# Attention's row sums from a further weight column and squares on ScalarE, last choices of 12 and 8 tiles, and a residual written from SBUF

## The chip, the cores and the metric

The kernel runs on one core of a Trainium2 chip. The metric is the time of one launch on the device, in microseconds (us): the median of several runs, as measured beside the runs of other kernels on the same chip. One execution is also recorded by the hardware profiler; the profile tables below come from that one.

## What is computed

The reference is a "macaron" block on x of 4 x 2048 tokens with 256 features, in float32: a mixture-of-experts layer, an attention layer and the same mixture again, each on a layer norm of its input and each added to x.

```python
x = x + 0.5 * ffn(layernorm(x), router_w, wg, wu, wd)
x = x + attn(layernorm(x), Wq, bq, Wk, bk, Wv, bv, Wo, bo)
x = x + 0.5 * ffn(layernorm(x), router_w, wg, wu, wd)

# attn: 16 heads of 16; the keys are a softmax of q, and k's projection is unused
q = softmax(heads(x @ Wq + bq), -1) * s
k = softmax(q, axis=-2) * s              # over the tokens
out = (q @ (k^T v)) @ Wo + bo            # a 16x16 context per head

# ffn: 8 experts, each token to its best 2, at most 1280 tokens per expert by weight
logits = x @ router_w.T ; top 2 of softmax, weights made to sum to 1
out[token] += weight * ((silu(x @ wg[e]) * (x @ wu[e])) @ wd[e])
```

## The kernel before

The 8192 tokens are 64 tiles of 128 (T = 64, 16 tiles per batch). The program has five stages that follow one another: a first router with its route (to about 113 us), the first experts (to 893), attention with the second router (to 1137), the second route (to about 1197), the second experts (to 1989). Each engine works through its own instructions in order. In the routers, routes, experts and attention that order is written out by hand for TensorE (PE), VectorE (DVE), ScalarE (ACT) and GpSimd (POOL), by the order of the calls; the transfers on SyncE's queue (SP) are placed by the scheduler.

**First router and route.** `first_router` (L1156) loads x into `xw` (128 partitions, 64 tiles, 280 columns: 256 of x, 8 of weights, 16 factors), computes each tile's logits and, for all 64 tiles at once, the choice of two experts (`choose`, L191). `write_rows` (L257) writes the rows of 280 to DRAM, from which the experts later gather. `route` (L260) finds for each expert the weight at which its capacity is reached, by 30 bisection steps of 1.32 us that pass between VectorE (L291, L296 to L298) and TensorE (L290, L292), and then the slot of each token: two scans on VectorE (L310, L319), one product (L320), four transposes on TensorE ("back", L326), and shifts (L328 to L335). Ahead of these transposes stand 14 filler matmuls of 128 columns (`stay_busy`, L158, called in L323), which wait for nothing but the matmuls before them. `RowList` (L357 to L416) turns the slots of the first expert into a list of rows, and GpSimd gathers them (L470). The first instruction of `RowList` on VectorE (L357, "hi") writes memory that the router's tiles held, so it waits for all transfers out of them. The first layer's residual, `acc`, is set to x by four transfers from DRAM to DRAM (L1245), and the experts' results are added to it.

**Experts.** Each of 16 chunks runs some 640 matmuls of 128x320 (L561, L764); TensorE is busy throughout. They start when the first rows are gathered.

**Attention** (L916). `acc` is loaded into `xw` in pairs of tiles, and a loop of 44 steps (L1105, LAST = 44) handles a pair of tiles at several ages in each step. In step i, by the order of calls:
- `project` and `largest` of pair i-1: q = x Wq by 8 matmuls ("qp", L949), scaled and shifted on VectorE (L957), its maxima (L962), its router columns copied (L963), the maxima subtracted on GpSimd (L964). The right-hand side has W1 = 264 columns: 256 of Wq and 8 of the router, so that the router's logits of x come with q.
- `keys` of pair i-3 (ScalarE, L981 twice, L983), `exp` and `share` of pair i-2 (ScalarE L967; sum and reciprocal on VectorE, L971 and L973; product on GpSimd, L974).
- `stats` of pair i+1 for attention's own layer norm (VectorE L933, L934; GpSimd L169, L170).
- `turn_q` of pair i-3 and `turn_x` of pair i: four transposes each on TensorE (L992, L941) and a copy on ScalarE (L994, L943).
- `add_y` of pair y = i-12: attention's output by 8 matmuls of 264 columns ("py", L1062), again with the router's logits.
- `sums` of pair i-3: products of keys and x over the batch's tokens, 8 matmuls ("pc", L1004).
- `choose_on`: a few instructions of a choice that is under way, then `take_y` (L1070): the output is added to `xw` on VectorE (L1072), both tiles get their statistics (L1074), every second pair is stored, and every second pair `norm_of` (L172) turns the statistics of four tiles into `rstd` and `shift`: four small VectorE instructions (L182 to L185), and on GpSimd `deviation` (L169, L170) and three more (L187 to L189). When a group of tiles is complete, its choice is queued.

After each batch (16 tiles, 8 pairs) `context_1` to `context_4` turn the sums into a matrix that maps q to the output: a reciprocal on VectorE (L1015), scalings (L1017, L1018), transposes ("trg", L1026), products ("ctx", "mops"). The groups of choices are 16, 16, 12, 16 and 4 tiles. In the last 8 steps only outputs and choices are left. Two PSUM buffers take turns for the outputs there.

The places that the change touches, with what is fixed by hand in them:

```python
            for n in (NJ, NJ, NJ - 4, NJ, 4):                                   # L1083, NJ = 16
...
                if i < LAST - PB - 2:                                           # L1145, PB = 8
                    choose_on(2)
                if has(y):
                    take_y(y, ps)
                if i >= LAST - PB:
                    choose_on({LAST - 3: 0, LAST - 2: 5, LAST - 1: 3}.get(i, 4))
            while choosing:
                for k in reversed(range(len(choosing))):
                    choose_on(1, k)
```

The whole functions:

Of the kernel before, what the change touches and what calls it, by code (L numbers as in the profile page):

```python
# [9 lines left out]
F32 = mybir.dt.float32  # L10
# [4 lines left out]
ALU = mybir.AluOpType  # L15
# [12 lines left out]
def macaron_kernel(  # L28
# [129 lines left out]
    def stay_busy(ps, n, cols=BANK):  # L158

        for _ in range(n):  # L160
            nc.tensor.matmul(ps[:, :cols], ident, row_of_ones[:, :cols], start=True, stop=True)
# [4 lines left out]
    def deviation(var, n, pool, dst, scale=1.0):  # L166

        ve = pool.tile([P, NJ], F32, tag="ve", name="ve", bufs=4)
        nc.gpsimd.tensor_scalar(ve[:, :n], var, scale, EPS, ALU.mult, ALU.add)  # L169
        nc.gpsimd.tensor_tensor(dst, ve[:, :n], spread(minus_half, [P, n]), ALU.pow)  # L170
# [89 lines left out]
    def route(w, pool, ppool, beside=iter(())):  # L260

        FULL = [P, GT * P]

        def new(name, dtype=F32):
            return pool.tile(FULL, dtype, name=name)

        def one(name, dtype=F32, n=1):
            return pool.tile([P, n], dtype, name=name)  # L270

        ps = ppool.tile([P, GT, P], F32, tag="turn", name="turn", bufs=1)
        by_group = w.rearrange("p e (g r) -> p r (e g)", r=GT)
        for r in range(GT):
            nc.tensor.transpose(ps[:, r, :], by_group[:, r, :], ident)
        wt = new("wt")
        nc.vector.tensor_copy(wt, ps.rearrange("p r q -> p (r q)"))

        cand, low, high = one("cand", I32), one("low", I32), one("high", I32)
        cand_f = cand.bitcast(F32)
        part = one("part", F16)
        above, tie = new("above", F16), new("tie", F16)
        nc.vector.memset(cand, 1 << 29)
        for bit in range(29, -1, -1):

            reach = ppool.tile([P, 4], F32, tag="cnt", name="reach", bufs=2)
            nc.tensor.matmul(reach[:, :1], group4, short, start=True, stop=False)  # L290
# [24 lines left out]
        nc.vector.tensor_tensor(need_t, need, cnt[:, 2:3], ALU.subtract)  # L315
        nc.vector.scalar_tensor_tensor(off, off, float(-1 - NOWHERE), cnt[:, 1:2], ALU.add, ALU.add)
        nc.vector.scalar_tensor_tensor(tie, St, need_t, tie, ALU.is_le, ALU.mult)
        nc.vector.tensor_tensor(above, above, tie, ALU.add)
        nc.vector.tensor_tensor_scan(St, row_of_ones, above, 0.0, ALU.mult, ALU.add)  # L319
        nc.vector.scalar_tensor_tensor(St, St, off, above, ALU.add, ALU.mult)  # L320


        stay_busy(ppool.tile([P, GT, P], F32, tag="turn", name="turn", bufs=1)[:, 0, :], 14, P)  # L323
        ps = ppool.tile([P, GT, P], F32, tag="turn", name="back", bufs=1)
        for r in range(GT):
            nc.tensor.transpose(ps[:, r, :], St[:, r * P : (r + 1) * P], ident)  # L326
        slot = pool.tile([P, E * T], I16, name="slot")
        nc.vector.tensor_scalar(  # L328
            slot.rearrange("p (q r) -> p q r", r=GT), ps.rearrange("p r q -> p q r"),
            float(NOWHERE), None, ALU.add,  # L330
        )
        nc.vector.tensor_scalar(
            slot_hi.rearrange("p e t -> p (e t)"), slot, 7, None, ALU.logical_shift_right
        )
        nc.vector.tensor_scalar(slot_lo.rearrange("p e t -> p (e t)"), slot, P - 1, None, ALU.bitwise_and)  # L335
        nc.gpsimd.tensor_scalar(behind_lo, slot_lo, -1.0, 0.5, ALU.mult, ALU.add)
# [509 lines left out]
                if i0 + CH == ST:  # L846
                    load_expert(e + 2, wpool, weights)

    W1 = D + E

    att_weights = []

    def attention_weights(pool, ppool):
# [18 lines left out]
        nc.sync.dma_start(out=boT, in_=bo.rearrange("(c p) -> p c", p=P))  # L872
        nc.sync.dma_start(out=box[:, 0:D], in_=bo.partition_broadcast(P))
        yield
        nc.gpsimd.tensor_copy(wqx[:, :, D:], wrx[:, :, :E])
        for w in (wqx[:, :, 0:D], wvx):
            ps = ppool.tile([P, 2 * D], F32, tag="turn", name="means", bufs=1)
            for c in range(DC):
# [17 lines left out]
        for k in range(DC):  # L896
            for c in range(DC):
                nc.tensor.matmul(
                    ps[:, k * E : (k + 1) * E], woT[:, c, k * P : (k + 1) * P], wqx[:, c, D:],
                    start=(c == 0), stop=(c == DC - 1),  # L900
                )
            yield
        nc.scalar.copy(wox[:, :, D:], ps[:, : DC * E].rearrange("p (k e) -> p k e", k=DC))
        yield
        ps = ppool.tile([P, 2 * D], F32, tag="turn", name="bor", bufs=1)
        for c in range(DC):
            bob = pool.tile([P, P], F32, tag="bob", name="bob", bufs=2)
            nc.scalar.mul(bob, ones, boT[:, c : c + 1])
            nc.tensor.matmul(ps[:, :E], bob, wqx[:, c, D:], start=(c == 0), stop=(c == DC - 1))
            yield  # L910
        nc.scalar.mul(box[:, D:], ps[:, :E], 1.0 / H)
        nc.gpsimd.tensor_scalar(box[:, 0:D], box[:, 0:D], 1.0 / H, None, ALU.mult)
        nc.gpsimd.tensor_scalar(mask, heads, QSCALE * QSCALE, None, ALU.mult)
        att_weights.extend((wqx, wvx, wox, bqs, bvT, box, mask))
# [1 line left out]
    def attention(xw, w, to, weights, pool, ppool):  # L916
# [3 lines left out]
        PB = NJ // 2  # L920
        NP = T // 2
        xT, qp, qs, zs, eks, qT, mo, pcs = {}, {}, {}, {}, {}, {}, {}, {}
        st3 = pool.tile([P, T, 6], F32, name="st3")
        ring = []
        for k in range(4):
            r = pool.tile([P, 2, D + 1], F32, name=f"xs{k}")
# [143 lines left out]
        def take_y(i, ps):  # L1070
            xs = xw[:, 2 * i : 2 * i + 2, 0:W1]
            nc.vector.tensor_tensor(xs, xs, ps[:, :, 0:W1], ALU.add)  # L1072
            for t in (2 * i, 2 * i + 1):
                nc.vector.bn_stats(st3[:, t, :], xw[:, t, 0:D])  # L1074
            t = 2 * i + 2 - JL
            if t % JL == 0:
                stored.append(nc.sync.dma_start(out=out_tiles[:, t : t + JL, :], in_=xw[:, t : t + JL, 0:D]))
            if i % 2:
                norm_of(st3, slice(2 * i - 2, 2 * i + 2), pool)


            stop = 0
            for n in (NJ, NJ, NJ - 4, NJ, 4):  # L1083
                stop += n
                if 2 * i + 2 == stop:
                    ts = slice(stop - n, stop)
                    choosing.append((ts, choose(xw, w, ts, pool)))

        def choose_on(n, which=0):

            while len(choosing) > which and n:
                ts, steps = choosing[which]
                n -= 1
                if next(steps, 0) == 0:
                    write_rows(xw, to, ts)
                    choosing.pop(which)

        def has(i, n=NP):
            return 0 <= i < n

        LAST = NP + PB + 4
        with tc.manual_schedule(engines=ENGINES):
            stay_busy(ppool.tile([P, 2, 2 * D], F32, tag="py", name="py", bufs=1)[:, 0, :], 7)
            stats(0, 2)
            for i in range(LAST):  # L1105
# [38 lines left out]
                    sums(i - 3)  # L1144
                if i < LAST - PB - 2:  # L1145
                    choose_on(2)
                if has(y):
                    take_y(y, ps)
                if i >= LAST - PB:

                    choose_on({LAST - 3: 0, LAST - 2: 5, LAST - 1: 3}.get(i, 4))
            while choosing:
                for k in reversed(range(len(choosing))):
                    choose_on(1, k)
# [57 lines left out]
    with tc.tile_pool(name="w1", bufs=2) as wpool:  # L1212
        weights, ws = {}, {}
        with tc.tile_pool(name="r1", bufs=1) as pool, tc.tile_pool(name="r1p", bufs=2, space=PSUM) as ppool:
# [5 lines left out]
            with tc.manual_schedule(engines=ENGINES):  # L1220
# [14 lines left out]
                steps = attention_weights(pool, ppool)  # L1235
                next(steps)
                first_router(xw, w, pool, ppool)
                for b in range(B):
                    write_rows(xw, rows[0], slice(b * NJ, (b + 1) * NJ))
                steps = chain(weight_sums(nc.gpsimd, 0, wpool, weights, ws, 0, 1), steps)  # L1240
                route(w, pool, ppool, steps)
                for _ in steps:
                    pass
        for b in range(B):
            nc.sync.dma_start(out=acc[b * N : (b + 1) * N, :], in_=x_in[b])  # L1245
        load_expert(1, wpool, weights)

        with tc.tile_pool(name="f1", bufs=1) as pool, tc.tile_pool(name="f1p", bufs=2, space=PSUM) as ppool:
# [55 lines left out]
```

## Time and profile before

| what | before |
|---|---|
| median of 3 runs | 1992.83 us (1991.8 to 1993.83) |
| profiled execution, its time | 1991.23 us |
| profiled execution, span of the instructions | 1989.5 us |
| busy: PE / DVE / ACT / POOL | 93% / 70% / 46% / 52% of the span |
| first rows gathered, first and second experts | 113.6 us, 1199.6 us |
| start of attention, start of the second route | 897.6 us, 1136.9 us |
| statistics of the outputs (DVE L1074) | 64 instructions, 24.1 us busy |
| TensorE's clock | 0.50 from 36.5 to 97.9 us and from 1128.8 to 1183.4 us, mostly 1.00 otherwise |

The span runs from the first instruction to the last; the execution's own time is 1.7 us longer. "Busy" is the time in which an engine had an instruction in work; a busy TensorE need not be at full speed, since its clock is granted in steps of one half and one. In a row of instructions the two numbers are the start and the length; "xN" merges N in a row, and where instructions overlap in the pipeline a single one's length is longer than the distance to the next one. In brackets stands how long the engine was idle ahead of it, and which work ended that wait. A chain follows from the last instruction back to what released each one.

### The profile page before, as it was taken

Reading aid. Unit: us, or ns where it says so; the run is one execution under the profiler, and the core shown is the slowest. Engines: PE = TensorE matmul, PEld = TensorE weight load, DVE = VectorE, ACT = ScalarE, POOL = GpSimd, SP = SyncE. Lnnn points to the kernel's source line nnn. Section 1 sums busy time; section 2 is a strip of 40 time slices with the busy share of each in tenths; the row PEclk is TensorE's granted clock in tenths of the full one; section 3 lists DMA queues with packets and bytes.
Section 4 is the critical chain, followed back from the end, with each engine's and each line's share of the span. In section 5 each row is a group of like instructions: output and inputs, shape, how many; then the busy total and the mean of one; then the engine's idle time right before and its main releaser. Section 6 shows DMA issues by size and latency. Waiting matters only on the chain.

```text
span 1989.5 us, 25361 instructions
## 1 busy us (share of the span) xinstructions
PE 1843.9 (93%) x8812; PEld 1341.8 (67%) x8812; DVE 1386.9 (70%) x2539; ACT 922.4 (46%) x2269; POOL 1031.8 (52%) x1019
## 2 busy tenths in 40 slices
PE   6479999999999999999999528999999999999997
PEld 5347777777777777777888425777777777777776
DVE  7856767676767676647788885676767666676763
ACT  5045455555646463325444105554646373737332
POOL 4335555555555555535556324555555555555552
PEclk8589999999999999999999858999999999999999
DMA  9911323222222221125012541222222223232121
GB/s 339 332 30 28 92 34 86 59 61 71 50 71 49 71 50 28 28 25 172 25 40 89 187 142 29 71 50 71 49 71 50 71 50 79 41 95 30 31 29 19
DMA packets 99936, 148.85 MB, mean 75 GB/s; under 512 B 7512, under 2 KB 86368, under 8 KB 99680
## 3 DMA queue, kind: packets, MB, share of 16 engines
q1 hardware_dynamic: 69072, 103.29, 15.3%
q0 software_dynamic: 30720, 43.93, 13.8%
q8 instruction: 70, 1.15, 0.3%
q14 instruction: 58, 0.48, 0.1%
q10 hardware_dynamic: 16, 0.01, 0.0%
HBM read 99.49 MB, written 56.10 MB: 78 GB/s over the span
## 4 chain that ended last, share of the span: by engine, by line
PE 88%; DVE 6%; issue 3%; POOL 1%; ACT 1%; DMA 1%; POOLq 0%; DVEq 0%; ACTq 0%; SPq 0%
PE mm L561 49%; PE mm L764 23%; PE qp L949 2%; PE pc L1004 2%; PE tr L496 2%; PE py L1062 2%; PE back L716 2%; DVE above L291 2%; PE ix L396 1%; PE mm L822 1%; PE tr L1168 1%; DVE cand L298 1%; PE trq L992 1%; PE trx L941 1%; PE lg L1177 0%
## 5 line engine op out<-in xcount | busy, mean ns | idle before, releaser
L561 PE MATMUL mm<-xs,ws 128*128 128x320 f32 x1536 | 476.9, 433 | 2.8 <-DVE u L502 1.8
L505 POOL TENSOR_TENSOR ct<-ct 128x320 f32<-128x320 f32 x360 | 339.6, 943 | 187.9 <-DVE ct L592 164.4
L561 PEld LDWEIGHTS mm<-xs,ws 128*128 128x128 f32 x1536 | 284.3, 190 | 111.9 <-DVE u L502 2.9
L502 DVE TENSOR_TENSOR ct<-u,mm 128x640 f32<-128x640 f32 x256 | 209.9, 820 | 177.2 <-PE mm L561 166.0
L502 DVE TENSOR_TENSOR ct<-ct,mm 128x640 f32<-128x640 f32 x288 | 236.0, 819 | 73.7 <-PE mm L561 72.8
L470 POOL DMA_INDIRECT r<-rows,ixs x160 | 156.9, 981 | 235.2 <-ACT eo L697 172.8
L764 PE MATMUL mm<-ct,wds 128*128 128x320 f32 x960 | 278.1, 432 | 0.0
L589 ACT ACTIVATE ct<-ct 128x960 f32<-128x960 f32 (+2 forms) x192 | 141.7, 738 | 293.1 <-DVE ct L502 293.1
L390 ACT ACTIVATE lo<-from_below,behind_lo 128x129 f16<-128x129 f32 x896 | 272.9, 396 | 0.0
L764 PEld LDWEIGHTS mm<-ct,wds 128*128 128x128 f32 x960 | 179.2, 190 | 72.0 <-DVE ct L502 3.3
L764 PE MATMUL mm<-ct,wdt 128*128 128x320 f32 x720 | 213.5, 433 | 0.0
L698 POOL DMA_INDIRECT acc<-eo,ixs x80 | 127.7, 1596 | 142.9 <-ACT eo L697 124.9
L698 POOL DMA_INDIRECT out_dram<-eo,ixs x80 | 127.6, 1595 | 142.9 <-ACT eo L697 124.9
L561 PE MATMUL mm<-xsT,wgt 128*128 128x320 f32 x512 | 184.8, 443 | 0.0
L561 PE MATMUL mm<-xsT,wut 128*128 128x320 f32 x512 | 180.7, 435 | 0.0
L592 DVE TENSOR_TENSOR ct<-ct 128x640 f32<-128x640 f32 (+1 forms) x128 | 160.8, 1256 | 21.7 <-ACT ct L589 21.7
L502 DVE TENSOR_TENSOR u<-p,mm 128x640 f32<-128x640 f32 x128 | 105.1, 821 | 93.0 <-PE mm L561 80.6
L764 PEld LDWEIGHTS mm<-ct,wdt 128*128 128x128 f32 x720 | 132.1, 190 | 47.5
L561 PE MATMUL mm<-xsT,ws 128*128 128x320 f32 x512 | 158.7, 432 | 0.0
L598 ACT COPY p<-mm 128x640 f32<-128x640 f32 x128 | 88.4, 690 | 147.1 <-PE mm L561 147.1
L697 ACT ACTIVATE eo<-back,r 128x256 f32<-128x256 f32 x150 | 64.9, 478 | 152.7 <-PE back L716 152.7
L561 PEld LDWEIGHTS mm<-xsT,wut 128*128 128x128 f32 x512 | 97.7, 191 | 40.7 <-issue 0.8
(234 smaller groups left out, 2803.7 us busy)
## 6 DMA issues: line engine op xcount, KB each, us to landing
wgt<-in_L_ffn_wg_dram SPq DMA_DIRECT2D x16, 1024.0 KB, 4.9
wut<-in_L_ffn_wu_dram SPq DMA_DIRECT2D x16, 1024.0 KB, 7.2
wdt<-in_L_ffn_wd_dram SPq DMA_DIRECT2D x16, 1024.0 KB, 5.4
rows<-xw SPq DMA_DIRECT2D x7, 2240.0 KB, 19.4
xw<-in_L_attn_x_dram SPq DMA_DIRECT2D x16, 512.0 KB, 9.3
out_dram<-xw SPq DMA_DIRECT2D x16, 512.0 KB, 2.9
xw<-acc SPq DMA_DIRECT2D x15, 512.0 KB, 8.6
r<-rows,ixs POOLq DMA_INDIRECT x160, 2.8
```

Source lines behind the costliest of these rows:

```text
L291: nc.vector.tensor_scalar(above, wt, cand_f, 0.0, ALU.is_ge, ALU.add, accum_out=part)
L390: nc.scalar.activation(lo[:, t, :], from_below, AF.Sign, bias=at, scale=1.0)
L470: nc.gpsimd.indirect_dma_start(out=r, out_offset=None, in_=src[:, :], in_offset=bass.IndirectOffsetOnAxis(ap=lists[e][:, i : i + 1], axis=0),)
L502: nc.vector.tensor_tensor(o, a, b, op)
L505: nc.gpsimd.tensor_tensor(o, a, b, op)
L561: nc.tensor.matmul(ps, a, b, start=start, stop=True, skip_group_check=not start)
L589: nc.scalar.activation(h(p)[:, qs, :], h(p)[:, qs, :], AF.Silu)
L592: engine.tensor_tensor(h(p)[:, qs, :], h(p)[:, qs, :], hT(p)[:, qs, :], ALU.mult)
L598: nc.scalar.copy(p1, ps)
L697: nc.scalar.mul(eo, ps, got[k][i][:, D + e : D + e + 1])
L698: ins = nc.gpsimd.indirect_dma_start(out=dst[:, :], out_offset=bass.IndirectOffsetOnAxis(ap=lists[e][:, i0 + i : i0 + i + 1], axis=0), in_ ...
L764: nc.tensor.matmul(ps, a(p), b(p), start=(p == 0 and not more), stop=(p == NF - 1), skip_group_check=more)
```

## The change

- A further column of -1/256 is put into the right-hand side of q (W1 = 265), and carried through Wo and its bias as the router's columns are. The matmuls of q and of the output so give minus the mean of each row beside the logits; it is added up in `xw` (column 264) like them.
- `bn_stats` and `norm_of` leave `take_y`. A new function `square_y` has ScalarE square the rows with that mean as bias and sum them (accumulator output), and GpSimd makes `rstd` and `shift` of four tiles from it. In the middle of attention it is called for the pair before (one step later than the add), in the last 8 steps for the pair just added. The queueing of a complete group's choice moves with it.
- The groups of choices become 16, 16, 12, 12 and 8 tiles, and the number of their instructions taken in the last steps is set anew.
- 8 filler matmuls instead of 14 in both routes.
- `acc` is written from `xw` in SBUF, ahead of the rows on SP's queue, instead of copied from x in DRAM. In the new order of SP's transfers the rows come next, and the weights of expert 1, which were ahead of the rows, behind them.

```diff
-        stay_busy(ppool.tile([P, GT, P], F32, tag="turn", name="turn", bufs=1)[:, 0, :], 14, P)
+        stay_busy(ppool.tile([P, GT, P], F32, tag="turn", name="turn", bufs=1)[:, 0, :], 8, P)
...
-    W1 = D + E
+    W1 = D + E + 1
...
-        nc.gpsimd.tensor_copy(wqx[:, :, D:], wrx[:, :, :E])
+        nc.gpsimd.tensor_copy(wqx[:, :, D : D + E], wrx[:, :, :E])
+        nc.gpsimd.memset(wqx[:, :, D + E :], -1.0 / D)
...
-            for t in (2 * i, 2 * i + 1):
-                nc.vector.bn_stats(st3[:, t, :], xw[:, t, 0:D])
             t = 2 * i + 2 - JL
             if t % JL == 0:
                 stored.append(nc.sync.dma_start(out=out_tiles[:, t : t + JL, :], in_=xw[:, t : t + JL, 0:D]))
+
+        def square_y(i):
+
+            for t in (2 * i, 2 * i + 1):
+                square = pool.tile([P, D], F32, tag="square", name="square", bufs=2)
+                nc.scalar.activation(
+                    square, xw[:, t, 0:D], AF.Square, bias=xw[:, t, W1 - 1 : W1], accum_out=squares[:, t : t + 1]
+                )
             if i % 2:
-                norm_of(st3, slice(2 * i - 2, 2 * i + 2), pool)
+                ts = slice(2 * i - 2, 2 * i + 2)
+                deviation(squares[:, ts], 4, pool, rstd[:, ts], 1.0 / D)
+                nc.gpsimd.tensor_tensor(shift[:, ts], xw[:, ts, W1 - 1], rstd[:, ts], ALU.mult)
...
-            for n in (NJ, NJ, NJ - 4, NJ, 4):
+            for n in (NJ, NJ, NJ - 4, NJ - 4, 8):
...
                 if i < LAST - PB - 2:
                     choose_on(2)
+                if has(y - 1) and i <= LAST - PB:
+                    square_y(y - 1)
                 if has(y):
                     take_y(y, ps)
                 if i >= LAST - PB:
-
-                    choose_on({LAST - 3: 0, LAST - 2: 5, LAST - 1: 3}.get(i, 4))
+                    square_y(y)
+                if i >= LAST - PB:
+
+                    choose_on({LAST - 5: 0, LAST - 4: 0, LAST - 1: 6}.get(i, 4))
...
                 first_router(xw, w, pool, ppool)
+                for t in range(0, T, NJ):
+                    nc.sync.dma_start(out=acc_tiles[:, t : t + NJ, :], in_=xw[:, t : t + NJ, 0:D])
                 for b in range(B):
                     write_rows(xw, rows[0], slice(b * NJ, (b + 1) * NJ))
...
-        for b in range(B):
-            nc.sync.dma_start(out=acc[b * N : (b + 1) * N, :], in_=x_in[b])
         load_expert(1, wpool, weights)
```

More of the change, by code (lines that the diff above doesn't have):

```diff
@@ L898, in attention_weights @@
                 nc.tensor.matmul(
-                    ps[:, k * E : (k + 1) * E], woT[:, c, k * P : (k + 1) * P], wqx[:, c, D:],
+                    ps[:, k * (E + 1) : (k + 1) * (E + 1)], woT[:, c, k * P : (k + 1) * P], wqx[:, c, D:],
                     start=(c == 0), stop=(c == DC - 1),
@@ L902, in attention_weights @@
             yield
-        nc.scalar.copy(wox[:, :, D:], ps[:, : DC * E].rearrange("p (k e) -> p k e", k=DC))
+        nc.scalar.copy(wox[:, :, D:], ps[:, : DC * (E + 1)].rearrange("p (k e) -> p k e", k=DC))
         yield
@@ L908, in attention_weights @@
             nc.scalar.mul(bob, ones, boT[:, c : c + 1])
-            nc.tensor.matmul(ps[:, :E], bob, wqx[:, c, D:], start=(c == 0), stop=(c == DC - 1))
+            nc.tensor.matmul(ps[:, : E + 1], bob, wqx[:, c, D:], start=(c == 0), stop=(c == DC - 1))
             yield
-        nc.scalar.mul(box[:, D:], ps[:, :E], 1.0 / H)
+        nc.scalar.mul(box[:, D:], ps[:, : E + 1], 1.0 / H)
         nc.gpsimd.tensor_scalar(box[:, 0:D], box[:, 0:D], 1.0 / H, None, ALU.mult)
@@ L922, in attention @@
         xT, qp, qs, zs, eks, qT, mo, pcs = {}, {}, {}, {}, {}, {}, {}, {}
-        st3 = pool.tile([P, T, 6], F32, name="st3")
+        squares = pool.tile([P, T], F32, name="squares")
         ring = []
```

## The prediction

> **What bounds the kernel now.** I read the page's chain by engine first, then the busy times of stretches, then the chain inside attention and the timelines of both routes.
>
> ```profile
> PE 88%; DVE 6%; issue 3%; POOL 1%; ACT 1%; DMA 1%; POOLq 0%; DVEq 0%; ACTq 0%; SPq 0%
> ```
>
> TensorE carries 88% of the chain, but the two expert stages (113 to 893 us and 1200 to 1989 us) are where most of it lies, and the change does not touch them. What it can win lies in the rest. Busy time of engines in two stretches of attention (length, then PE, PEld, DVE, ACT, POOL, each with its count, granted clock, DMA share, GB/s):
>
> ```profile
> 1060.00:1080.00 20.00, 20.00 (x108) 17.51 (x107) 17.38 (x52) 8.48 (x18) 9.76 (x18) 1.00 0.16 54
> 1120.00:1130.00 10.00, 5.84 (x27) 4.64 (x25) 9.15 (x31) 0.31 (x1) 5.17 (x14) 0.94 0.77 262
> ```
>
> In the middle of attention TensorE is full; in its tail VectorE is full and ScalarE empty. The chain in order of time (start, us, what) says the same at closer range:
>
> ```profile
> 998.98 0.60 DVE xw L1072
> 999.60 0.75 DVE st L1074 x2
> ...
> 1003.29 0.66 PE trg L1026 x4
> ...
> 1053.66 0.75 DVE st L1074 x2
> ...
> 1057.35 0.66 PE trg L1026 x4
> ...
> 1118.43 0.75 DVE st L1074 x2
> 1119.18 0.61 DVE xw L1072
> 1119.82 0.76 DVE st L1074 x2
> ...
> 1136.88 1.10 PE turn L275 x4
> ```
>
> Statistics on VectorE (st L1074) stand on the chain before the context transposes of two batches (trg) and all through the tail up to the second route (turn L275). Last, the first route's timeline:
>
> ```profile
> 92.07 6.16 PE L161 MATMUL turn<-row_of_ones,ident 128*128 128x128 f32 x28
> 95.94 0.75 DVE L320 SCALAR_TENSOR_TENSOR St<-St,nums,above 128x512 f32<-128x512 f32 x1
> 98.29 0.66 PE L326 MATMUL back<-ident,St 128*128 128x128 f32 x4
> 100.95 0.69 DVE L357 TENSOR_TENSOR hi<-counts,slot_hi 128x1024 f16<-128x1024 int16 x1 [0.75 <-POOL behind_lo L336]
> ```
>
> The slots are ready at 96.69, but the transposes start at 98.29, behind the 14 fillers (two records each).
>
> **The change, part by part.** The profiled execution took 1991.23 us (span 1989.5), the median of the runs is 1992.83; I sum on the first and carry the difference over.
>
> *Statistics off VectorE.* Per pair of tiles two statistics instructions (0.75 together) go, and per second pair four small ones (0.17+0.16+0.16+0.16 by duration; they take 0.56 from the first to the next instruction): 0.70+0.28 = about 1.0 us of VectorE per step. In full steps TensorE hides this: a step costs it 1.78 (qp) + 0.88 (two transposes) + 1.78 (py) + 1.74 (pc) = 6.18 us, and no VectorE saving shortens that. It counts where VectorE is late:
> - Batch boundary at 1003 us: the last pc ends at 999.57, but the reciprocal that starts the context waits for the statistics until 1000.27. Gain 0.7, after which the order of ScalarE (context scaling, two scalings, two exponentials, copy) still leaves TensorE some 0.4 idle.
> - Boundary at 1057: VectorE spends 6.3 to 6.7 us a step while it also does choices, above 6.18, so it has drifted behind; TensorE stands 0.26 + 1.77. With 1.0 us less it keeps pace, and 0.4 stays as at the other boundary: gain 1.65.
> - Last boundary: TensorE waits 1.12 + 0.19 at 1094 to 1096 for q, late because VectorE's z came late. Without the statistics its reciprocal is ready at 1092.5, GpSimd's multiplication at 1093.65, and TensorE runs on from 1093.7: 0.44+1.78+1.74 twice and 0.16 for the last result, so pc ends at 1101.8 instead of 1103.4: gain 1.65.
> - Tail of eight pairs: VectorE needs 1.40 a pair (adds 0.7, statistics 0.7) plus 0.28 plus the choices. Afterwards it needs 0.7 a pair, and TensorE's 1.78 a pair sets the pace: with two PSUM buffers the last py ends 14.4 us after the first starts, at 1123.8 if the first starts 1.65 before its 1111.04. Ahead of the last add stand 15 instructions of the second choice of 12, whose exponential ScalarE reaches only after the squares of the pair two before (1122.3). By these steps the last add is at 1125.8 rather than 1128.92, of which 1.65 is counted already: 1.5 more. The path behind the last add was 0.68+0.79+0.48 on VectorE and 1.5 to the choice's first instruction at 1132.40, 3.48 in all; it becomes 0.7 + two squares 1.3 + GpSimd's 0.2 and 1.05 with gaps, some 3.5. No change.
>
> *Last choices of 12 and 8 instead of 16 and 4.* The final choice of 4 tiles took 1132.40 to 1136.73, 4.33 us, shared with the end of the one of 16. One of 8 runs alone: 21 instructions at the 0.15 to 0.2 us of the neighbouring groups plus the exponential's trip, 3.6 to 4.5. Gain 0 to 0.7, I take 0.2.
>
> *Squares on ScalarE.* 64 squares with an accumulator output; the trace has no such operation. The nearest row is the scaling of 128x256, 504 ns, two of them in 0.91 (0.41 apart). The accumulator's read is unknown: VectorE's is 86 ns, a small ScalarE copy 185. So a pair costs 0.9 to 1.4; I take 1.3. ScalarE is busy 2.9 us of 6.18 in a step, so 4.2 afterwards. Queued behind the squares are the next step's two scalings and two exponentials; from the step's qp, its copies end at 3.5, the squares at 4.8 and the scalings at 5.7, while in the steps at 987 and 993 the first exponential waits for GpSimd until 5.9 anyway, and pc needs it only 4.5 us later. GpSimd's deviation waits for the squares, with the next subtraction behind it; but it comes after two multiplications and a deviation that end later than the squares. So nothing on the path, in either direction; GpSimd loses two operations (0.20, 0.23) per second pair. No table load is added in the changed order of instructions. Here a rule speaks against the change: the Trainium skill's "ScalarE: Activation LUTs", Rules for kernel authors, gives plain arithmetic to VectorE and not to ScalarE. Its price is that statistics at 0.34 apart beat squares at 0.65: counted in engine time, 64 x 0.31 = 20 us are lost. The row of 1120 to 1130 decides against it, since ScalarE is idle there (0.31 of 10) and the loss lies beside TensorE's work.
>
> *A 265th column.* 256 qp and 256 py matmuls get one column more. From pc's 257 columns (1.74 for eight) to qp's 264 (1.78) it is 0.7 ns a column, from 264 to 320 (387 to 433 ns) 0.8: 512 x 0.8 = 0.4 us lost, all on TensorE's path.
>
> *Fillers 14 to 8.* At 0.22 a record 16 records end at 95.6, before the slots, in the first route. The transposes then start at 96.8 but at half clock: four take 1.10 (turn L275, clock 0.50) instead of 0.66 at full clock. Net 1.0. In the second route the fillers end at 1185.06 with the slots at 1184.81: 0.25 won, 0.44 lost, so -0.2. The rule behind it is "TensorE: Matmul & The Clock Gate", Part 1: full clock needs one busy window of about 3.4 us, on a free-running phase. The trace agrees (0.50 until 97.9, then 1.00, in steps of 3.41). By the rule, 3.5 us of fillers fill a window only with lucky phase; then the 0.44 is not lost. I take it as lost.
>
> *Residual from SBUF.* Four writes move ahead of the rows on SP, and expert 1's three loads behind them. The rows' last packets land at about 100.4, and VectorE's hi starts at 100.95, after a 0.75 wait: either GpSimd's or the rows'. In the new order 3.1 MB less lie ahead of the rows, at about 0.33 MB/us 9 us earlier, so that the 0.75 goes too if it is theirs. hi's earliest time is then 99.25 and the first route wins 1.0 to 1.7. Below nothing: small 1 KB rows from SBUF could be slower than DRAM to DRAM; but loads of 1 KB rows ran at 340 GB/s, and 7 us of cover remain. Part of a gain goes back at the expert's start, where TensorE runs at half clock until a window passes: I take 1.3.
>
> Sum: 1.3 - 0.2 + 0.7 + 1.65 + 1.65 + 1.5 + 0.2 - 0.4 = 6.4 us.
>
> **The rivals.** *Half of it* (0.23): another wait takes the place of statistics at the boundaries, ScalarE's queue now carrying 1.3 us of squares ahead of the context's scaling, and the DVE/GpSimd hand-offs stay in step. Against it, ScalarE waited 3.7 and 4.9 us for the reciprocal there. Then the first route gives 1.0, the tail 1.3 and the boundaries 1.8, less 0.6: 3.5, near 1989.3.
> *Slower by the squares* (0.08): the accumulator's read serialises ScalarE. The tail gives it 1.78 a pair; from 0.9 us a square on, ScalarE sets the tail, each 0.1 costing 1.6 us over eight pairs, and from 1.3 the gain is used up. At 1.8 it would exceed a full step too (2.9+3.6 = 6.5): about +10, 2003. For it: no row shows such an operation. Against it: the kindred row's 0.41.
> *The copy doesn't move as it says* (0.04): SBUF writes are slow, rows land after 107 instead of 91, and the first route loses what the rest wins: 1991 to 1996.
>
> **How the numbers follow.** The likeliest, 0.65: 1992.83 - 6.4 = 1986.4. Its own bounds: the first route 0.7 to 1.9, boundaries 2.5 to 4.3, tail and choice 0.7 to 3, the rest -0.8 to -0.2, so 3 to 9 less; ends rarely meet: 1984 to 1989. The range 1983.3 to 1990.3 takes in the half case and a little luck of clock phase. 0.2% is 4 us, about what a measurement of this kernel can tell from no change. Faster: most of the first case and a fifth of the second, 0.68; same 0.22; slower 0.10.
>
> **What would show it.** Right: no wait over 0.6 us before trg at the second and third boundary; py in the tail back to back, 64 within 14.5 us; turn L275 some 5 us earlier after the start of attention; hi at about 99.3 us; rows landing near 92. Wrong: squares over 0.9 us apart, ScalarE without gaps in the tail, GpSimd's q later than in before, or back L326 at half clock followed by a later hi.

## The result, and the profile after

The changed kernel takes 1985.36 us (median of 6 runs, 1983.98 to 1987.7), the kernel before 1992.65 us beside it (6 runs, 1991.07 to 1993.83). The ratio is 0.9964 with a 95% interval of 0.9954 to 0.9975: 7.3 us less, with 5.0 to 9.2 in the interval. 1986.4 us was forecast, 6.4 less.

The profiled execution of the changed kernel is the slowest of its six: 1987.7 us (span 1985.9). Against the profiled one of before (1991.23) that is 3.5 us, not 7.3; a part of the other half shows in the profile's clock column further down. First the chain by engine on its page:

```profile
PE 89%; DVE 6%; issue 1%; ACT 1%; POOL 1%; DMA 1%; POOLq 0%; DVEq 0%; ACTq 0%; SPq 0%
```

The chain looks as before, since the experts fill it; only "issue" fell, from 3% to 1%. The same two stretches of attention (length, then PE, PEld, DVE, ACT, POOL, granted clock, DMA share, GB/s):

```profile
1060.00:1080.00 20.00, 20.00 (x104) 17.40 (x103) 14.15 (x38) 10.64 (x29) 9.55 (x14) 1.00 0.29 95
1120.00:1130.00 10.00, 4.82 (x22) 3.75 (x20) 6.51 (x27) 4.54 (x17) 4.22 (x10) 0.96 0.96 328
```

VectorE went from 17.38 to 14.15 in the middle and from 9.15 to 6.51 in the tail; ScalarE took up 2.2 and 4.2 us. The chain through attention, in order of time (line numbers of attention are one higher than before: xw L1073 is the addition; square L1082 is the new work):

```profile
999.72 0.18 DVE rc L1016
...
1002.75 0.66 PE trg L1027 x4
...
1051.47 0.34 DVE p L205
...
1051.83 0.38 DVE w L205
1052.21 0.54 DVE xw L1073
...
1055.69 0.66 PE trg L1027 x4
...
1121.27 0.72 DVE xw L1073
1122.08 1.09 ACT square L1082 x4
...
1127.11 1.10 ACT square L1082 x4
...
1134.07 1.10 PE turn L275 x4
```

The statistics are gone from the three places where they stood. What is late in their stead: at 1003 nothing on VectorE; at 1057 still VectorE, with the addition behind two instructions of a choice (p, w) and attention's own layer norm; in the tail the additions, each behind TensorE's pair, and two squares of 1.1 us a pair at its end. The first route:

```profile
92.19 3.76 PE L161 MATMUL turn<-row_of_ones,ident 128*128 128x128 f32 x16
96.06 0.75 DVE L320 SCALAR_TENSOR_TENSOR St<-St,nums,above 128x512 f32<-128x512 f32 x1
96.96 1.09 PE L326 MATMUL back<-ident,St 128*128 128x128 f32 x4 [1.01 <-DVE St L320]
99.39 0.62 POOL L336 TENSOR_SCALAR behind_lo<-slot_lo 128x512 f32<-128x512 int16 x1 [27.62 <-DVE slot_lo L335]
99.49 1.05 DVE L357 TENSOR_TENSOR hi<-counts,slot_hi 128x1024 f16<-128x1024 int16 x1 [0.19 <-DVE slot_lo L335]
```

The fillers end (95.95) before the slots are ready (96.81), the transposes run at half clock (1.09 for 0.66), and hi starts at 99.49 instead of 100.95. The rows' last packets land at 88.9, 11.4 us earlier.

**Additions as a ruler.** The 32 additions of attention's outputs (xw<-xw,py) come at the same distances in every profile of one kernel, at nearly all steps to 0.05 us, except where a half-clock window falls in (3.41 us in which TensorE is granted half its clock): then all later ones shift by some 1.7 us (1.4 in two of seven profiles). So their starts, counted from the first one, compare kernels without the noise of single runs. Below are the second profiles of both kernels, taken later on another chip (their expectations stand among the experiments). They have no half clock in attention until the last addition:

| start after the first addition, us | before | changed | difference |
|---|---|---|---|
| 7th addition (last full step) | 37.04 | 37.16 | +0.12 |
| 15th (last one ahead of the boundary at 1057) | 91.08 | 90.21 | -0.87 |
| 21st | 133.05 | 130.59 | -2.46 |
| 24th (first behind the last boundary) | 148.31 | 145.89 | -2.42 |
| 32nd and last | 167.02 | 162.79 | -4.23 |
| turn L275, the second route's start | 174.98 | 170.55 | -4.43 |

From the first addition on, attention wins 4.43 us. The first profile of the changed kernel shows less because a half-clock window (1108.65 to 1112.07) fell into its tail.

### The profile page after: what moved, and what is told of

Read it like the earlier page. It is cut to its first block, busy times and chain, and to the rows that moved or that the text cites. A ratio compares the mean times of both kernels' runs of the same rounds, so it can differ in the third digit from the quotient of the medians.

```text
span 1985.9 us, 25303 instructions
## 1 busy us (share of the span) xinstructions
PE 1843.6 (93%) x8788; PEld 1342.6 (68%) x8788; DVE 1354.1 (68%) x2411; ACT 954.4 (48%) x2397; POOL 1025.2 (52%) x988
## 4 chain that ended last, share of the span: by engine, by line
PE 89%; DVE 6%; issue 1%; ACT 1%; POOL 1%; DMA 1%; POOLq 0%; DVEq 0%; ACTq 0%; SPq 0%
PE mm L561 49%; PE mm L764 23%; PE py L1063 3%; PE pc L1005 3%; PE qp L950 3%; DVE above L291 2%; PE tr L496 2%; PE back L716 2%; PE ix L396 1%; PE mm L822 1%; DVE cand L298 1%; PE tr L1181 1%; PE trq L993 1%; PE trx L942 1%; PE reach L292 1%
## 5 line engine op out<-in xcount | busy, mean ns | idle before, releaser
L697 ACT ACTIVATE eo<-back,r 128x256 f32<-128x256 f32 x150 | 64.9, 478 | 152.7 <-PE back L716 152.7
```

The lines of the kernel that those rows point to most:

```text
L697: nc.scalar.mul(eo, ps, got[k][i][:, D + e : D + e + 1])
```

## The experiments

Ratios are to the kernel before, timed on the same chip; intervals are at 95%. In us, 0.001 is 2.0.

**The change in three parts, each alone.**

```diff
# first: route alone
-        stay_busy(..., 14, P)
+        stay_busy(..., 8, P)
...
+                for t in range(0, T, NJ):
+                    nc.sync.dma_start(out=acc_tiles[:, t : t + NJ, :], in_=xw[:, t : t + NJ, 0:D])
...
-            nc.sync.dma_start(out=acc[b * N : (b + 1) * N, :], in_=x_in[b])
# second: statistics alone (all that the change does for column and squares)
-    W1 = D + E
+    W1 = D + E + 1
...
-                nc.vector.bn_stats(st3[:, t, :], xw[:, t, 0:D])
...
+                    square_y(y - 1)
# third: groups alone, with bn_stats
-            for n in (NJ, NJ, NJ - 4, NJ, 4):
+            for n in (NJ, NJ, NJ - 4, NJ - 4, 8):
...
-                    choose_on({LAST - 3: 0, LAST - 2: 5, LAST - 1: 3}.get(i, 4))
+                    choose_on({LAST - 5: 0, LAST - 4: 0, LAST - 1: 6}.get(i, 4))
```

> The kernel before, with the two edits around the first route alone: 8 fillers in place of 14, and the residual copied from SBUF ahead of the row writes. Main theory (most of the gain is the statistics leaving VectorE): between -1.3 and 0 us, about -0.5; the route's last gather comes about 1.1 us earlier, as in the changed kernel, but the experts that follow start on a half clock and give a part back. Rival (the gain is the earlier route and the residual that is no longer read): -4 us or more. The row packets end some 11 us earlier under both.

> The kernel before, with the 265th column, the squares on ScalarE and the later deviation alone; 14 fillers, the residual from DRAM and the groups 16, 16, 12, 16, 4 stay as before. Main theory: -4 to -6.5 us, most of the 7.3 us of the whole change. Rival (route and residual): -3 us or less. Rival (regrouping of the last choices is needed for the gain, since the four tiles' last choice is what it was before): -2 to -3 us. In the profile, if the main theory holds: the additions of the tail stand as many us apart as the PE's pairs, 1.79, and the waits before trg at the second and third boundary are as in the whole change.

> The kernel before, with the last groups of 12 and 8 tiles and their new placing alone; the statistics stay on VectorE (bn_stats). Main theory: within 0.7 us of the kernel before: VectorE sets the pace of the tail by addition and statistics together, and a choice of 8 in place of 4 at the end costs about what the other 8 tiles give. Rival (regrouping carries the gain): -3 us or more. A third possibility: with the statistics still on VectorE, the placing doesn't fit and it costs +1 us or more.

Measured: route alone 0.9993 (0.9985 to 1.0001); statistics alone 0.9979 (0.9970 to 0.9988); groups alone 1.0003 (0.9995 to 1.0011). So -1.4, -4.2 and +0.6 us: the statistics carry most, and the rivals that gave the gain to the route or the groups fall. But the three add up to -5.0 and not to -7.2, so one part may be worth more beside another, though the intervals would allow for chance. The ruler names it. With the statistics alone the 24th addition stands at 145.89 as in the changed kernel, so all that the boundaries give comes from the statistics; with the groups alone it stands where it stood before (150.02, less 1.71 of one half clock, for 148.31). In the tail the statistics alone bring four additions 1.79 apart, each behind TensorE's pair, as was expected, and the last one 165.59 after the first, one half clock of 1.68 included, so 163.91 without; the changed kernel has 162.79. **The groups are worth 1.1 us once the statistics are gone**, while with bn_stats they cost 0.6 (169.29 less 1.71 is 167.58, for 167.02). A choice of 12 that is done earlier helps only when VectorE has time for it.

**Statistics and groups without the route** (the changed kernel with 14 fillers and the residual from DRAM), and the changed kernel once more on the same chip:

> The changed kernel with 14 fillers and the residual from DRAM: statistics and groups changed, the first route as before. Theory: 0.5 to 1.5 us slower than the changed kernel on this chip, and 1 to 2 us faster than the squares alone were against their kernel before (0.9979), since with the statistics gone the groups of 12 and 8 save 1.1 us in the tail. Rival (groups worth nothing here either; the route makes the rest): 2.5 us or more slower than the changed kernel. In its profile the last addition comes 13.99 us after the eighth from the end, as in the changed kernel, if no half clock falls there.

> The changed kernel once more, beside the two that follow on one chip. The additions of attention's outputs, read one by one from the profiles, make the change worth 4.2 us in attention and 5.1 us in all when no half clock of TensorE falls into it; the medians differed by 7.3. Theory (the rest is half clocks: each costs 1.7 us, and the gaps at the old boundaries draw them more often): the median again 6 to 8 us below the kernel before, the fastest runs of both only 4.5 to 5.5 apart, and the runs of the kernel before spread wider. Rival (a lasting gain that the profiles of single executions hide): the fastest runs are 7 apart as well.

Measured: 0.9970 (0.9958 to 0.9982) without the route, 0.9964 (0.9951 to 0.9978) with it; medians 1990.04 (6 runs) and 1987.55 (5 runs), lowest runs 1987.44 and 1987.39. The means of these few runs are 1.3 apart, the medians 2.5, which is the rival's figure: the times cannot tell. The profile does: the last addition comes 13.99 us after the eighth from the end (164.41 less 150.42, behind that kernel's half clock), as in the changed kernel (162.79 less 148.80). So attention's gain needs neither of the route's edits.

For the changed kernel the median is 7.4 below the kernel before again, with lowest runs 5.45 apart (1992.84 and 1987.39), and the kernel before spreads wider (4.4 us for 2.4, though with 26 runs for 5). These times fit the theory, with few runs; its reason, that the old boundaries draw half clocks more often, is not borne out by the count of half clocks below.

**The tail's pace.** Additions at the tail's end in the second profile of the kernel before:

```profile
1118.01 0.69 DVE L1072 TENSOR_TENSOR xw<-xw,py 128x528 f32<-128x528 f32 x1
1120.07 0.69 DVE L1072 TENSOR_TENSOR xw<-xw,py 128x528 f32<-128x528 f32 x1
...
1123.45 0.70 DVE L1072 TENSOR_TENSOR xw<-xw,py 128x528 f32<-128x528 f32 x1
1127.82 0.64 DVE L1072 TENSOR_TENSOR xw<-xw,py 128x528 f32<-128x528 f32 x1
```

And in the second profile of the changed kernel:

```profile
1115.39 0.71 DVE L1073 TENSOR_TENSOR xw<-xw,py 128x530 f32<-128x530 f32 x1 [1.08 <-PE py L1063]
1117.18 0.71 DVE L1073 TENSOR_TENSOR xw<-xw,py 128x530 f32<-128x530 f32 x1 [1.08 <-PE py L1063]
1118.97 0.71 DVE L1073 TENSOR_TENSOR xw<-xw,py 128x530 f32<-128x530 f32 x1 [1.08 <-PE py L1063]
1121.99 0.70 DVE L1073 TENSOR_TENSOR xw<-xw,py 128x530 f32<-128x530 f32 x1
1124.01 0.70 DVE L1073 TENSOR_TENSOR xw<-xw,py 128x530 f32<-128x530 f32 x1
```

Before, none of these four waits for TensorE and the last starts 4.37 us after the one ahead. Now VectorE waits 1.08 for each of three pairs and the distance is 1.79, TensorE's pace, until the choice of 12 fills the last two distances.

**Cover of the squares.** Each square of the changed kernel is done twice.

```diff
+                nc.scalar.activation(
+                    again, xw[:, t, 0:D], AF.Square, bias=xw[:, t, W1 - 1 : W1], accum_out=unused
+                )
```

> The changed kernel with every square computed twice on ScalarE, the second result unused: 1.1 us more of ScalarE a pair. Theory (ScalarE lies under cover in the full steps, and only the tail sees it): in the full steps nothing (ScalarE then has about 5.1 of 6.2 us), in the tail a pair needs 2.2 us of ScalarE for the PE's 1.79, and 7 pairs make +2 to +3.5 us. Rival (ScalarE's queue sits between DVE's results and TensorE's next step in the full steps as well): +8 us or more, 0.2 us or more in each of the 64 steps. Rival (ScalarE has room in the tail, too): within 0.7 us of the changed kernel.

Measured: 0.9981 (0.9974 to 0.9987), 3.4 us less gain than the changed kernel's 0.9964 on other chips. Two stretches, middle and tail:

```profile
980.00:1000.00 20.00, 20.00 (x104) 17.37 (x103) 13.26 (x36) 14.90 (x44) 11.56 (x19) 1.00 0.16 54
1110.00:1120.00 10.00, 10.00 (x47) 8.46 (x46) 6.28 (x18) 9.15 (x38) 5.43 (x12) 1.00 0.59 196
```

In the middle ScalarE rises to 14.90 of 20 us (11.32 in the changed kernel) and TensorE stays full; by the ruler the 24th addition comes 0.2 later. In the tail ScalarE is nearly full (9.15 of 10), the last addition comes 2.1 later (164.92) and turn L275 another 1.0. So the squares lie under cover in the steps but for 0.2 us, and double ones cost the tail 2.9. The theory's figure (2 to 3.5) holds.

**The column's price.** One, and two, unused columns in the kernel before.

```diff
-    W1 = D + E
+    W1 = D + E + 1        # the other kernel: + 2
```

> The kernel before, which carries a 265th column of weights through attention that nothing uses (its values are computed and thrown away). The prediction put it at +0.4 us (0.8 ns a column and matmul). Theory from the profile of the changed kernel (its steady step took 6.20 us for 6.17): +0.6 to +1.0 us, 1.6 ns a column and matmul. Both differ by less than the spread of single runs, so the length of the steady step in the profile counts too: 6.18 us or less by the prediction, 6.20 by the theory.

> The kernel before with two unused columns more in place of one. If an odd width is what costs, the steady step is as long as with 265 columns or shorter (6.18 to 6.20 us); if every column costs the same 1.6 ns, it is 6.23 us; by the prediction's 0.8 ns, 6.20.

Measured: 0.9998 (0.9990 to 1.0007) for one; 1994.88 us in a single run for two, beside a median of 1995.26. Six steps from the first addition take 37.02 with 264 columns, 37.16 with 265, 37.24 with 266: 0.023 a step for the first column and 0.013 for the second, 1.5 and 0.8 ns a column and matmul record (16 records a step; each matmul of the program stands as two records in the profile, and the counts of matmuls ahead are of records). A second column costs too, so it is not the odd width alone. But the last addition comes at 167.29 with two columns for 167.05, 0.12 for each: where TensorE waits for VectorE anyway, the longer matmul is free. The steps ahead of the first addition come on top. From the experts' last result (eo, L697) to the first addition, in profiles without a half clock there, it is 66.8 and 67.1 us with 264 columns, 67.2 to 67.3 in four kernels with 265; with a half clock there 68.8 to 69.0 in three, and 68.9 to 69.1 in four. That is 0.1 to 0.3 more in the means. So one column costs 0.1 to 0.4 us in all, no more than the forecast and below the theory.

**The residual's path.** The changed kernel with the copy from DRAM, but 8 fillers:

```diff
-                    nc.sync.dma_start(out=acc_tiles[:, t : t + NJ, :], in_=xw[:, t : t + NJ, 0:D])
+            nc.sync.dma_start(out=acc[b * N : (b + 1) * N, :], in_=x_in[b])
```

> The changed kernel with the residual copied from the input in DRAM again. Prediction: the copy from SBUF moves the row packets and is worth nothing in time, since the gathers wait for the route. Theory: within 0.5 us of the changed kernel; the row packets end near 100 us again and the load of the second expert's weights comes earlier. Rival (reading 8.4 MB less matters to the experts' weights): +1 us or more.

Measured: 0.9971 (0.9960 to 0.9982), 1.4 less gain than the changed kernel had on other chips, with intervals that overlap. What its profile says is sharper. With the residual from DRAM the row packets land at 99.38 us and hi starts at 100.03:

```profile
96.99 1.09 PE L326 MATMUL back<-ident,St 128*128 128x128 f32 x4 [1.01 <-DVE St L320]
...
100.03 0.69 DVE L357 TENSOR_TENSOR hi<-counts,slot_hi 128x1024 f16<-128x1024 int16 x1 [0.70 <-POOL behind_lo L336]
```

Here the fillers alone bring the transposes forward, and hi then stands and waits. The wait is put down to GpSimd there, but in the profile of the groups alone the same line names the rows:

```profile
102.35 0.69 DVE L357 TENSOR_TENSOR hi<-counts,slot_hi 128x1024 f16<-128x1024 int16 x1 [2.25 <-DMA rows<-xw]
```

Last row packet and start of hi in the nine profiles with the residual from DRAM: 99.01 and 99.72, 99.14 and 99.82, 99.38 and 100.03, 99.59 and 100.23, 99.98 and 100.64, 100.16 and 100.82, 100.30 and 100.95, 100.36 and 101.00, 101.71 and 102.35, always 0.64 to 0.71 apart. So hi follows the rows, and the 0.75 wait of before was theirs, which the prediction had left open. The expectation's "worth nothing in time" (it was not the prediction's either, which put the residual into the first route's 1.3) was wrong: hi stands up to 2.25 us for the rows, and as long as it does, fewer fillers do not bring it forward. The residual with 14 fillers was not run.

**TensorE's clock.** Fillers in attention's gaps, in the changed kernel at the last boundary, and in the kernel before at all four:

```diff
# changed kernel
+                    stay_busy(spare[:, 0, :], 2, P)
                     context_4(b3)
+                    stay_busy(spare[:, 0, :], 5, P)
# kernel before: these two, and at the other boundaries
+                    stay_busy(spare[:, 0, :], 4, P)
                 if has(b3, B):
                     context_2(b3)
```

> The changed kernel, with 2 filler matmuls ahead of the last batch's context and 5 behind it, into a PSUM tile that is free there. In the profile of the changed kernel TensorE's granted clock was half from 1108.8 to 1112.2 us of the span, right where the tail's first pairs run. Theory A (the gaps of PE before the tail open the clock's half step, in each run): about 1.5 us faster than the changed kernel, 1983.5 to 1984.5 us against the kernel before at 1992.7. Theory B (the dip falls there by chance of phase, and most runs of the changed kernel don't have it): no gain, between 0 and +0.7 us beside the changed kernel, the fillers' own 0.5 us. Either way no half clock between 1100 and 1120 us in its profile if fillers prevent it.

> The kernel before with fillers in attention's batch boundaries: 4 matmuls of 128 columns ahead of the context's transposes of three batches (about 0.5 us at full clock in a gap of 0.7 to 2.0), and 2 and 5 at the last one, nothing else. Theory (half clocks drawn by the gaps at the boundaries are part of the difference): 1 to 2.5 us faster than the kernel before in the median, with the same fastest runs, and no half clock at 1057 or 1110 us. Rival (their place is chance, and fillers don't change it): between 0 and 1 us slower.

> The kernel before once more, for a second profile of it: where its half clocks fall, and whether the additions stand as far apart as in the first (167.05 us from the first to the last without one). Theory: the same distances, plus 1.4 to 1.7 us wherever a half clock falls; one at 1057 or 1110 us is likely, since four of the five kernels that keep the statistics on VectorE were seen with the same gaps and two of them with a half clock at 1057.

Measured: changed kernel with fillers 0.9963 (0.9949 to 0.9976), no half clock at the last boundary in its profile, and no gain that could be told from the changed kernel's 0.9964. Kernel before with fillers 0.9991 (0.9984 to 0.9997), 1.8 us faster (0.6 to 3.2), with the same additions (167.02) and no half clock in attention, as the theory had it. The second profile of the kernel before (1991.98 us) has the same additions and no half clock either, so the likely one at 1057 did not come. How a half clock is drawn is seen in the exact windows of the clock. Route alone (length, PE, PEld, DVE, ACT, POOL, clock, DMA share, GB/s):

```profile
1054.02:1057.43 3.41, 1.65 (x13) 1.29 (x13) 2.80 (x9) 3.26 (x7) 1.61 (x4) 1.00 1.06 341
1057.43:1060.85 3.42, 3.42 (x11) 2.70 (x9) 1.26 (x5) 2.44 (x6) 2.38 (x4) 0.50 0.00 0
```

Second profile of the kernel before, same gap, other phase:

```profile
1052.57:1055.98 3.41, 1.69 (x11) 1.03 (x9) 2.82 (x9) 2.54 (x6) 1.70 (x3) 1.00 1.07 352
1055.98:1059.40 3.42, 3.13 (x20) 2.88 (x21) 1.94 (x7) 3.15 (x7) 3.01 (x4) 1.00 0.21 66
```

The program has the same instructions in this gap; only the window's edges fall elsewhere. TensorE is busy for 1.65 us of one window and 1.69 of the other. The first is followed by a window at half clock, the second isn't. In the 14 profiles, between 940 and 1115 us, all 13 windows with TensorE busy for up to 48% were followed by a half clock, and of those with 49% or more only one (at 49%). In the additions a half clock cost 1.4 to 1.7 us, up to half a window.

## Why the forecast held, step by step

| step | forecast | measured |
|---|---|---|
| first route | +1.3 | +0.6 |
| second route | -0.2 | +0.6 |
| boundary at 1003 | +0.7 | +0.5 |
| boundary at 1057 | +1.65 | +1.1 |
| last boundary | +1.65 | +0.8 |
| tail and groups | +1.5 and +0.2 | +2.0 |
| 265th column | -0.4 | -0.1 to -0.4; all but 0.1 to 0.3 of it inside the rows above |
| sum | 6.4 | 5.6, or 5.3 to 5.5 with the column's part ahead of the first addition |

The boundaries' rows are the starts of trg, counted from the first addition: 41.42 before and 40.92 after, 95.48 and 93.86, then the 24th addition. The mechanism was right in the main: statistics off VectorE give 3.3 (2.4 at the boundaries, 0.9 in the tail), the largest share, and the groups, which pay only once the statistics are gone, 1.1. The total came out well by luck: errors of size cancelled, with three steps put too high by 2.1 (first route, last two boundaries: 4.6 forecast, 2.5 measured), and the second route and the tail too low by 1.1.

- **Boundary at 1057.** The step said that VectorE would keep pace with 1.0 us less. It does not quite: the changed chain still runs through p, w and the addition, and trg still waits 0.94 us where I had named 0.6 as the sign (at 1003 it waits 0.41). The reciprocal comes 0.6 us after the batch's last pc has ended (1052.04 and 1051.46 in the changed kernel's second profile), about the gain that is missing. The forecast counted the statistics and left the choice's instructions out. The two waits, in the second profiles of before and after:

```profile
1056.27 0.66 PE L1026 MATMUL trg<-ident,g 128*128 128x128 f32 x4 [1.76 <-ACT qT L994]
```

```profile
1055.07 0.66 PE L1027 MATMUL trg<-ident,g 128*128 128x128 f32 x4 [0.94 <-ACT qT L995]
```

- **Last boundary.** "TensorE runs on from 1093.7" failed: it still waits, on the chain below (changed kernel, second profile). After qp the line goes through VectorE to the next py. The choice's b, 128x16, takes 0.95 there where 0.16 is usual.

```profile
1085.82 1.81 PE qp L950 x8
...
1087.72 0.89 DVE q L958 x2
...
1088.63 0.69 DVE m L963
...
1089.40 0.60 DVE z L972
...
1090.66 0.95 DVE b L205
...
1091.89 0.63 DVE xw L1073
...
1092.56 2.06 PE py L1063 x8
```

- **Tail and groups.** 1.7 forecast, 2.0 measured (4.43 less 2.42), but split otherwise: the groups are 1.1 of it, not 0.2, and the statistics 0.9, not 1.5.
- **Squares.** 1.3 us a pair was taken, 1.1 came; the rival "slower by the squares" needed 0.9 us a square, they stand 0.50 apart. The rule that gives plain arithmetic to VectorE (the Trainium skill, "ScalarE: Activation LUTs", Rules for kernel authors) is outweighed here as the forecast said: doing the squares twice costs 0.2 us in all the full steps together.
- **First route.** The experts' first weight load on TensorE comes 1.2 us earlier: at 117.25 in the mean of five profiles with both route edits, 118.41 in eight with neither. Then 0.5 to 0.9 (0.6 in the mean of four chips) is given back (from that load to the experts' last result 774.46 before, 775.33 after, on one chip). The experts start at half clock and stay there until 120 to 124, whatever the kernel, so an earlier start means a longer stretch at half clock. By the clock's windows that accounts for 0.4 of the 0.6 in the mean; the rest is open. Hence 0.6 net, where 1.3 was forecast.
- **Second route.** The loss of 0.2 was a wrong sign, because the sum was made on one lucky phase. From turn L275 to the back transposes the kernels with 8 fillers take 48.0 to 48.1, those with 14 fillers 48.0 to 49.4. Statistics alone, an unlucky case, then the changed kernel's second profile:

```profile
1178.84 5.91 PE L161 MATMUL turn<-row_of_ones,ident 128*128 128x128 f32 x28
1182.72 0.75 DVE L320 SCALAR_TENSOR_TENSOR St<-St,nums,above 128x512 f32<-128x512 f32 x1
1184.81 0.66 PE L326 MATMUL back<-ident,St 128*128 128x128 f32 x4
```

```profile
1175.10 3.76 PE L161 MATMUL turn<-row_of_ones,ident 128*128 128x128 f32 x16
1178.97 0.75 DVE L320 SCALAR_TENSOR_TENSOR St<-St,nums,above 128x512 f32<-128x512 f32 x1
1179.87 0.63 PE L326 MATMUL back<-ident,St 128*128 128x128 f32 x4 [1.01 <-DVE St L320]
```

  At half clock 14 fillers last 5.9 us and hold the transposes 1.3 us past the slots; 8 never do. And in five of the six profiles with 8 fillers the transposes run at full clock (0.63; 1.09 in route alone), so the 0.44 that the forecast took as lost mostly wasn't. To the second experts' first weight load the means are 68.29 (eight profiles with 14) and 67.65 (six with 8): 0.6.

Of the median's 7.3 us, 5.3 to 5.5 are so accounted for. With the interval of 5.0 to 9.2 the rest can be chance; if it isn't, its cause stays open. The two second profiles differ by 4.4 us in all (1991.98 and 1987.55), since the routes gave this pair next to nothing; but that profile of before is also quicker than all 26 runs of before on its chip (1992.84 and up).

As far as twelve profiles show, half clocks in attention do not explain the rest. Without added fillers, the six profiles with the old statistics have three at about 952 (ahead of the first addition), two at 1057 and one at the last boundary; the six with the new ones have three, none and four. That is one per profile either way, 6 and 7 in all. It agrees with the 1.8 us that fillers save in the kernel before, but gives the change no gain.

## What to carry to other kernels

Work moved from a full engine to an idle one is worth what the *gaps* behind the full engine are long, less what stands next in its queue: list the instructions between the removed one and the waiting reader before crediting the whole gap. Edits interact: a regrouping that cost 0.6 us alone gave 1.1 once VectorE had time, and fewer fillers brought nothing while the rows came late. Where single runs spread by some us, compare the distances of a repeated instruction between profiles; here they agreed to 0.05 us at nearly all steps and showed each disturbance as a step.

## What the hardware showed that was not expected

- In attention the clock halved for a window of 3.41 us whenever TensorE had been busy for up to 48% of the window before (13 of 13), though the longest gap in these was 1.3 to 1.8 us (1.77 at 1057). The Trainium skill ("TensorE: Matmul & The Clock Gate", Why this matters for your kernels) warns of gaps above about 3 us; here shorter ones sufficed when they fell into one window, and in the same kernel they did in some profiles and not in others.
- A square with accumulator output has a second instruction in the profile, 0.19 us long, but the next square starts 0.50 after the first (which itself takes 0.51), so most of it overlaps.
- VectorE's b, 128x16, took 1.02 us beside GpSimd's product and 0.16 elsewhere in the same profile (changed kernel, second profile). The kernel before has the same meeting at 1087.

```profile
1038.72 0.16 DVE L205 TENSOR_TENSOR b<-b,rs 128x16 f32<-128x16 f32 x1
...
1090.52 1.06 POOL L975 TENSOR_TENSOR q<-q,rz 128x512 f32<-128x512 f32 x1
1090.59 1.02 DVE L205 TENSOR_TENSOR b<-b,rs 128x16 f32<-128x16 f32 x1
```

  It ends when GpSimd's instruction does (1091.6). The Trainium skill's "SBUF — State Buffer" (Who interferes with whom) names this pair, a VectorE instruction with two SBUF inputs and a GpSimd one that reads SBUF, as one that contends. hi in the first route may be a milder case: 1.05 beside behind_lo, 0.69 alone, so 0.36 of what the route won went there.
